# Scattering MoE results by node, keeping block marks, and adding index products on TensorE in a four-layer GNN with mixtures of experts

## The chip, the cores and the metric

The kernel runs on one core of a Trainium2 chip. The metric is device microseconds of one execution, the median of five runs. The engines are TensorE (PE, with its weight loads as PEld), VectorE (DVE), ScalarE (ACT), GpSimd (POOL) and SyncE (SP). DMAs are issued from SP's, ACT's and POOL's queues; a DMA whose rows go to or come from places given by a list of indices is an indirect DMA and is issued by POOL, 128 rows in each.

## The reference, cut to what matters

N = 3125 nodes hold rows of D = 256 floats. Eight layers follow one another, each added to the rows after a layer norm:

```python
x = x + L0_gnn(ln(x), edge_weight, src, dst)       # weighted sum over 50000 edges
x = x + L0_ffn(ln(x))      # 8 experts, top 2, hidden 512, relu
x = x + L1_gnn(ln(x))      # two graph attentions with 4 heads, W 256x256
x = x + L1_ffn(ln(x))      # tokens + 8 experts, top 2, hidden 256, gelu
x = x + L2_gnn(ln(x))      # normalised weighted sum, then a two-layer MLP
x = x + L2_ffn(ln(x))      # scores by a graph attention, 4 experts, top 2
x = x + L3_gnn(ln(x))      # two mean aggregations
x = x + L3_ffn(ln(x))      # 8 experts, top 2, hidden 1024, gelu
```

A mixture of experts (MoE) picks for each node the two experts e with the largest gate values and forms

```python
out[node] = w0 * (act(x[node] @ W1[e0] + b1[e0]) @ W2[e0] + b2[e0]) \
          + w1 * (act(x[node] @ W1[e1] + b1[e1]) @ W2[e1] + b2[e1])
```

The edges come sorted by dst. One layer of the kernel needs them in the other order too, by the block of 128 nodes to which src belongs.

## The kernel before, in words

The nodes lie in T = 25 tiles of P = 128; `X` in on-chip memory holds all of them. The stages run in the order of the layers; look preparation of edge lists comes first. The tile framework puts the instructions of each engine into an order when the program is built, and each engine then runs its own list in that order, with semaphores between them.

**The other graph's places (`own_places`, L1795 to L1820).** For 128 x 512 edge slots the kernel computes the slot in a table sorted by block. For each block b of 25 a mark (`op_B`: is the edge in block b, L1803) is scanned to a running count (`op_S`, L1804); the mark is used once and its buffer given back. In a second loop the mark is made again (L1816), multiplied with the count and the block's offset (`op_q`, L1817), and added to a sum `op_f` (L1819). All this is DVE's. `os_at` (L1820) is the result as integers.

**Sending the edge records (`own_send`, L1826).** 512 indirect DMAs on POOL write 128 edge records each to their places in the table `os_table`. They are handed out in small numbers among other stages' work: 21 in look, 5 x 8 while the first buckets are filled, two after each of 100 source steps of r0_gnn and 12 in its last 25 steps, three a chunk in r0_ffn (84), nine in each of four attention tails, three or four a chunk in r1_ffn (98), and 21 behind r1_ffn. `os_mark` (L1838, in `settle`) is a read of the table ahead of a branch. `own_load` reads the table back as `fa_rec`.

**r0_gnn.** The 25 destination tiles are taken in five groups of five. For each group 25 source steps follow: `r_hs` and `r_hd` (L1549) on DVE, products `r_pw` (L1553) on PE, the copy `r_wt` (L1557) on ACT, the sums `r_pa` (L1521) on PE, and an addition to X (L1522). The dense blocks `r_wt` also go to `mats` in DRAM. Beside the first four groups the fields of the next group's buckets are filled, one bucket in five steps (`bf_rh`, L1473). In the fifth group the steps of the following MoE's gate are mixed in.

**The gate (`mix_group`, `mix_send`).** Token tiles are taken in six groups (5, 5, 5, 5, 4, 1): a layer norm into `gh_xn` (two buffers; L191, L206 on ACT for r0_ffn), gate values, the top two experts with weights `gd_w`, and places `gd_at`. For each expert there is a region of rows in the DRAM tensor `regions`; each tile's rows are sent there by two indirect DMAs on POOL (L869, 50 in each MoE). `clear` (L100) zeros `regions` at the beginning by 26 DMAs of 1 MB on SP.

**The experts (`gated`).** Three MoEs (r0_ffn, r1_ffn, r3_ffn) use it. Chunks of 256 rows of a region are taken: rows `gx_xs` (L987) and weights `gx_w` arrive by SP; PE turns the rows over (`gx_pt`, L997), DVE copies them (`gx_xt`, L999); PE and ACT compute `gx_h` (L1004, L1005); and one chunk later `second` computes `gx_po` (L974) and, on DVE, `gx_ys` (L976). A DMA on ACT's queue (L977) puts the 256 result rows at place k x 256 of `ff_results`, in the order of chunks. 28 chunks run always; four more stand in a branch that this input does not take. For the places, 25 x 8 small arrays (`gd_adj`, `gd_q`, `gd_qs`) turn `gd_pos` into rows of `ff_results`, and three DMAs of 1 MB write zeros to the four chunks in the branch.

**Bringing the results back (`mix_result`, L1035).** For each tile and each of the two experts an indirect DMA (L360, `gb_y`) on POOL collects 128 rows of `ff_results`, and DVE adds `w * y` to X:

```python
y = pool.tile([P, D], F32, name="gb_y")
self.gather(y, m.results, m.at[i][:, t:t + 1])
nc.vector.scalar_tensor_tensor(self.X[:, t, :], y, m.w[i][:, t:t + 1], self.X[:, t, :], op0=OP.mult, op1=OP.add)
```

In r0_ffn and r1_ffn this is done in the next stage (r1_gnn, r2_gnn) group by group, followed by the norm and the first product (`hd_hx` there, `r_xw` here) of the group. In r3_ffn it is the end of the program, with the output DMAs.

In r1_gnn the two attentions collect rows by 832 indirect DMAs on POOL (L360, `ad_rows` from `r_rows`).

## Time and profile before

| what | value |
|---|---|
| median of five runs | 4864.8 us (4862.15 to 4866.09) |
| the profiled execution | 4864.93 us, of it the traced span 4863.1 us |
| PE busy | 3445.5 us (71%), 20909 instructions |
| DVE busy | 2862.3 us (59%), 9396 instructions |
| ACT busy | 2152.2 us (44%) |
| POOL busy | 2103.1 us (43%), 2107 instructions |
| os_table, L1826 POOL | 512 sends, 551.2 us, mean 1077 ns |
| regions rows, L869 POOL | 150 sends, 150.3 us, mean 1002 ns |
| gb_y, L360 POOL | 150 gathers, 154.8 us, mean 1032 ns |
| ad_rows from r_rows, L360 POOL | 832 gathers, 820.1 us, mean 986 ns |
| mean granted TensorE clock | 0.845 |

Busy times are shares of one span that has many stages with different limits; a stage has to be read by its own stretch. In the lines of the profile, `L360 POOL DMA_INDIRECT gb_y<-ff_results,gd_at x150` is a line of the kernel, an engine, an operation, what it writes and reads, and how many there are; `<-` behind a time names what ended the wait. Stretches are named by their bounds in us from the start of the span, as in 84:124. A row of the table by stage has the length, the busy time of each engine with its number of instructions, the granted PE clock, the share of the DMA engines' time and the GB/s that they moved.

### The profile page before, as it was taken

The page shows a single profiled execution, that of the slowest core. Times are in us where ns is not written, and L with a number is a line of the kernel's source. Part 1 is how long each engine was busy: PE and PEld are TensorE (multiplying, and loading weights), DVE is VectorE, ACT ScalarE, POOL GpSimd, SP SyncE. Part 2 cuts the span into 40 slices and gives each one's busy share as a digit, 9 for nine tenths or more (in the row PEclk, how much of TensorE's full clock was granted, in tenths as well). Part 3 has the DMA queues.
Part 4 walks back from the last instruction along what each step waited for, and adds up shares of the span by engine and source line. Part 5 has one row for each costly group of instructions (what it writes and reads, how often), then busy time and mean ns, then how long its engine had stood idle before and what let it go on. Part 6 is the DMA issues. An engine that isn't in the chain of part 4 may idle for free. (4 is left out here: it accounts for less than half of the span.)

```text
span 4863.1 us, 66173 instructions
## 1 busy us (share of the span) xinstructions
PE 3445.5 (71%) x20909; PEld 2770.8 (57%) x20909; DVE 2862.3 (59%) x9396; ACT 2152.2 (44%) x5957; POOL 2103.1 (43%) x2107
## 2 busy tenths in 40 slices
PE   1299988934666445545637877677877999979993
PEld 1189976823444334434525766444545888868883
DVE  7988863255666457766337876567778785231112
ACT  3366552225766456666114987333334332112220
POOL 0586533357777577775573000277770000120003
PEclk9699988966777667776878988788988999989996
DMA  1552226634545244443642222211110112325554
GB/s 58 167 167 96 96 106 196 219 109 135 145 140 145 66 134 136 131 129 89 190 132 94 109 82 82 54 36 32 36 30 6 67 62 81 104 95 199 187 193 132
DMA packets 329438, 543.00 MB, mean 112 GB/s; under 512 B 69070, under 2 KB 242002, under 8 KB 325872
## 3 DMA queue, kind: packets, MB, share of 16 engines
q1 hardware_dynamic: 213430, 354.48, 21.6%
q0 software_dynamic: 84032, 154.27, 12.1%
q10 hardware_dynamic: 31610, 29.84, 1.8%
q8 instruction: 173, 2.83, 0.2%
q14 instruction: 193, 1.58, 0.1%
HBM read 393.49 MB, written 145.37 MB: 111 GB/s over the span
## 5 line engine op out<-in xcount | busy, mean ns | idle before, releaser
L360 POOL DMA_INDIRECT ad_rows<-r_rows,fa_gi x832 | 820.1, 986 | 277.5 <-issue 241.3
L1826 POOL DMA_INDIRECT os_table<-os_rec,os_at x512 | 551.2, 1077 | 548.1 <-ACT gx_h L1005 152.4
L360 POOL DMA_INDIRECT ad_rows<-q_rows,own_gi x416 | 401.7, 966 | 633.5 <-DVE ad_hb L2104 510.4
L2213 ACT ACTIVATE ad_rows<-ad_rows 128x64 f32<-128x64 f32 x2544 | 617.0, 334 | 1.6
L2223 PE MATMUL ad_acc<-ad_rows,ad_hd 128*128 128x260 f32 x1664 | 519.7, 466 | 6.6 <-ACT ad_rows L2213 5.9
L869 POOL DMA_INDIRECT regions<-gh_xn,gd_at x150 | 150.3, 1002 | 738.8 <-PE r_pa L1654 544.9
L1654 PE MATMUL r_pa<-r_xs,r_cnt 128*128 128x257 bf16 (+1 forms) x3750 | 450.0, 273 | 0.9 <-ACT r_xs L1627 0.9
L1005 ACT ACTIVATE gx_h<-gx_pa,gx_bias 128x256 f32<-128x256 f32 x392 | 185.8, 474 | 571.3 <-PE gx_pa L1004 546.1
L2223 PEld LDWEIGHTS ad_acc<-ad_rows,ad_hd 128*128 128x128 f32 x1664 | 368.0, 233 | 73.6 <-ACT ad_rows L2213 11.2
L976 DVE TENSOR_TENSOR gx_ys<-gx_po,gx_b 128x256 f32<-128x256 f32 x168 | 70.6, 423 | 548.3 <-PE gx_po L974 528.6
L1654 PEld LDWEIGHTS <-r_cnt 128*128 128x128 bf16 x3750 | 362.2, 98 | 48.5 <-issue 0.2
L2126 PE MATMUL ad_pt<-ident,ad_e 128*4 128x128 f32 x75 | 26.2, 349 | 498.7 <-DVE ad_e L2123 407.5
L1004 PE MATMUL gx_pa<-gx_xt,gx_w 128*128 128x256 f32 x1568 | 364.7, 387 | 3.5 <-DMA gx_w<-in_L_ffn_W 2.3
L974 PE MATMUL gx_po<-gx_w,gx_h 128*128 128x256 f32 x1568 | 365.8, 379 | 0.0
L360 POOL DMA_INDIRECT gb_y<-ff_results,gd_at x150 | 154.8, 1032 | 482.8 <-SPq L126 438.9
L1004 PEld LDWEIGHTS gx_pa<-gx_xt,gx_w 128*128 128x128 f32 x1568 | 293.9, 192 | 68.0 <-DVE gx_xt L999 18.9
L974 PEld LDWEIGHTS gx_po<-gx_w,gx_h 128*128 128x128 f32 x1568 | 290.1, 190 | 38.1 <-ACT gx_h L1005 2.2
L1521 PE MATMUL r_pa<-r_xn,r_wt 128*128 128x257 f32 x1250 | 301.0, 386 | 14.3 <-ACT r_wt L1557 13.0
L2126 PEld LDWEIGHTS ad_pt<-ident,ad_e 128*4 128x4 f32 x75 | 6.1, 82 | 531.1 <-issue 497.7
L2600 PE MATMUL ss_sum<-r_xw,ss_wt 128*128 128x256 f32 x1250 | 290.0, 394 | 6.2 <-DMA ss_wt<-mats 6.2
L2600 PEld LDWEIGHTS ss_sum<-r_xw,ss_wt 128*128 128x128 f32 x1250 | 245.6, 198 | 41.7 <-issue 6.6
L2112 ACT CAST ad_hd<-ad_hb 128x2176 f32<-128x2176 bf16 (+1 forms) x50 | 98.4, 1968 | 355.0 <-PE ad_acc L2223 265.4
(573 smaller groups left out, 7133.9 us busy)
## 6 DMA issues: line engine op xcount, KB each, us to landing
gx_w<-in_L_ffn_W SPq DMA_DIRECT2D x56, 1024.0 KB
mats<-r_wt SPq DMA_DIRECT2D x25, 1600.0 KB
ss_wt<-mats SPq DMA_DIRECT2D x25, 1600.0 KB
gx_w<-in_L_ffn_W SPq DMA_DIRECT2D x56, 512.0 KB
regions<-zero SPq DMA_DIRECT2D x26, 1024.0 KB
ad_rb<-fa_relT SPq DMA_DIRECT2D x48, 544.0 KB
gx_xs<-regions SPq DMA_DIRECT2D x84, 256.0 KB
ff_results<-gx_ys ACTq DMA_DIRECT2D x84, 256.0 KB
```

The lines of the kernel that those rows point to most:

```text
L360: return self.nc.gpsimd.indirect_dma_start(out=out, out_offset=None, in_=table[:, :], in_offset=bass.IndirectOffsetOnAxis(ap=idx, axis=0))
L869: ins = nc.gpsimd.indirect_dma_start(out=self.regions[:, :], out_offset=bass.IndirectOffsetOnAxis(ap=m.at[i][:, t:t + 1], axis=0), in_=x, ...
L974: nc.tensor.matmul(po, h[:, f, j * P:(j + 1) * P], w2s[:, f, :], start=f == 0, stop=f == FC - 1)
L1004: nc.tensor.matmul(ps, w1s[:, c, f * P:(f + 1) * P], xt[:, c, :], start=c == 0, stop=c == DC - 1)
L1005: done = nc.scalar.activation(h[:, f, :], ps, act, bias=bias1[:, f, k:k + 1])
L1521: nc.tensor.matmul(pa, wt[:, i, :], xn[:, g * G + i, :], start=i == 0, stop=i == G - 1)
L1654: nc.tensor.matmul(pa[:, 0:n], c[:, u, :], xs[i][:, u, j, 0:n], start=u == 0 and j == 0, stop=u == T - 1 and j == 2)
L1826: i = nc.gpsimd.indirect_dma_start(out=s.table[:, :], out_offset=bass.IndirectOffsetOnAxis(ap=s.at[:, c:c + 1], axis=0), in_=s.rec[:, c, : ...
L2112: nc.scalar.copy(x.hd[:, :x.kb, :], x.hb[:, :x.kb, :])
L2213: i = nc.scalar.activation(v, v, AF.Copy, scale=x.rt[:, k, W4 + h:W4 + h + 1])
L2223: nc.tensor.matmul(x.acc, lhs[:, k, :], rhs[:, k, :], start=i == 0, stop=i == x.kb - 1)
L2600: nc.tensor.matmul(sums[t], wt[:, d, :], xw[:, d, :], start=d == 0, stop=d == T - 1)
```

## The change

1. Rows that go to `regions` get a 257th column, a number that holds the MoE, the node and the second of its two experts. It is made by three small DVE operations for each group in `mix_group`. `clear` and the loads of `gx_xs` have 257 columns too.
2. In `gated`, a new function `places` computes from that column, by seven small DVE operations for each chunk, at which row of a DRAM tensor of 8192 rows (4096 for each of the two experts of a node, in the order of nodes) each result belongs. `second` sends `gx_ys` there by two indirect DMAs for each chunk on POOL. The ACT DMA, the small arrays for the places and the zeros of the branch's chunks are gone; two small DMAs zero the 75 rows behind the last node.
3. `settle` also reads one element of the results, before the branch and after it.
4. `mix_results` brings the results back by plain DMAs on SP, two for each group of tiles and up to three groups ahead, in place of 50 indirect DMAs on POOL. The DVE additions are as before.
5. The numbers of `own_send` change: three instead of two after each of r0_gnn's first 100 steps, seven instead of nine in the attention tails, one a chunk instead of three or four in r1_ffn. With these all 512 are sent by the 27th chunk of r1_ffn, and the reads of `own_load` come ahead of r1_ffn's branch on SP.
6. `own_places` keeps its 25 marks, and the 25 products are added up by TensorE: a matmul with the identity for each, into one PSUM tile. `op_q` has two buffers.

```diff
-        self.regions = self.dram.tile([8 * RC, D], F32, name="regions")
+        self.regions = self.dram.tile([8 * RC, D + 1], F32, name="regions")
...
+            self.nc.sync.dma_start(self.landed, self.landing[0:1, 0:1])
...
+        e1 = hp.tile([P, TG, E], F32, name="gh_e1")[:, :G, :]
+        nc.vector.tensor_tensor(e1, s1, m.far[:, None, :].to_broadcast(all_), OP.mult)
+        nc.vector.tensor_reduce(rows[:, :, D], e1, AX.X, OP.add)
+        nc.vector.tensor_add(rows[:, :, D], rows[:, :, D], m.tag[:, gs])
...
-                    nc.scalar.dma_start(results[k * CH:(k + 1) * CH, :].rearrange("(j p) d -> p j d", p=P), y)
+                        i = nc.gpsimd.indirect_dma_start(
+                            out=results[:, :], out_offset=bass.IndirectOffsetOnAxis(ap=to[:, j:j + 1], axis=0),
+                            in_=y[:, j, :], in_offset=None, bounds_check=2 * HALF - 1, oob_is_err=False)
...
+                def places(k, xs):
+                    code = xs[:, :, D]
+                    ci_ = yp.tile([P, CJ], I32, name="gx_ci")
+                    nc.vector.tensor_scalar(ci_, code, float(-TAG * m.n), None, op0=OP.add)
...
+                    to = yp.tile([P, CJ], I32, name="gx_to")
+                    nc.vector.tensor_tensor(to, half, ci_, OP.add)
+                    return to
...
                         nc.vector.tensor_copy(xt, pt)
+                        to = places(k, xs)
...
-                        if k == 3:
-                            nc.scalar.dma_start(results[KA * CH:K * CH, :].rearrange("(q p) d -> p q d", p=P),
-                                                self.zero[:, None, 0:D].to_broadcast([P, (K - KA) * CJ, D]))
...
+    def mix_results(self, m, pool):
+        nc, ys = self.nc, []
+        groups = list(GROUPS)
+        def fetch():
+            g, n = groups.pop(0)
+            y = pool.tile([P, 2, TG, D], F32, name="gb_y")
+            for i in range(2):
+                nc.sync.dma_start(y[:, i, 0:n, :], m.results[i * HALF + g * P:i * HALF + (g + n) * P, :].rearrange("(t p) d -> p t d", p=P))
+            ys.append(y)
+        for g, n in GROUPS:
+            while groups and len(ys) < 3:
+                fetch()
+            y = ys.pop(0)
+            for t in range(n):
+                for i in range(2):
+                    nc.vector.scalar_tensor_tensor(self.X[:, g + t, :], y[:, i, t, :], m.w[i][:, g + t:g + t + 1],
+                                                   self.X[:, g + t, :], op0=OP.mult, op1=OP.add)
+            yield g, n
...
-                    self.own_send(2 if g < T // G - 1 else src % 2, done)
+                    self.own_send(3 if g < T // G - 1 else src % 2, done)
...
+            B = pool.tile([P, T, C], BF16, name="op_B")
+            for b in range(T):
+                nc.vector.tensor_scalar(B[:, b, :], blk, float(b), None, op0=OP.is_equal)
...
-                B = p2.tile([P, C], BF16, name="op_B")
-                nc.vector.tensor_scalar(B, blk, float(b), None, op0=OP.is_equal)
-                nc.vector.scalar_tensor_tensor(q, S[:, b, :], off[:, b:b + 1], B, op0=OP.add, op1=OP.mult)
-                if b:
-                    nc.vector.tensor_add(f, f, q)
-            nc.vector.tensor_scalar_add(s.at, f, NOWHERE)
+                q = p2.tile([P, C], F32, name="op_q")
+                nc.vector.scalar_tensor_tensor(q, S[:, b, :], off[:, b:b + 1], B[:, b, :], op0=OP.add, op1=OP.mult)
+                nc.tensor.matmul(acc, self.ident, q, start=b == 0, stop=b == T - 1)
+            nc.vector.scalar_tensor_tensor(s.at, drop, NOWHERE / 64.0, acc, op0=OP.mult, op1=OP.add)
...
-                self.own_send(9, i)
+                self.own_send(7, i)
...
-        self.gated(self.mix, "L1_ffn_w1", "L1_ffn_b1", "L1_ffn_w2", "L1_ffn_b2", AF.Gelu, send=3, more=2, tail=False)
+        self.gated(self.mix, "L1_ffn_w1", "L1_ffn_b1", "L1_ffn_w2", "L1_ffn_b2", AF.Gelu, send=1, tail=False)
```

## Prediction

> **What bounds it now.** The profiled execution took 4864.9 us (span 4863.1, the rest lies around it); the median of the runs is 4864.8, so the sum below is made against 4864.9. No engine bounds the whole span, so I read the table by stage first: the stretches that the change touches.
>
> ```profile
> core 0: us, PE busy (x) PEld busy (x) DVE busy (x) ACT busy (x) POOL busy (x), PEclk, DMA share, GB/s
> 84.00:124.00 40.00, 1.43 (x14) 1.06 (x14) 39.91 (x80) 1.61 (x3) 0.00 (x0) 1.00 0.31 92
> 200.00:280.00 80.00, 46.90 (x323) 42.56 (x323) 77.86 (x165) 60.25 (x166) 65.68 (x48) 0.75 1.00 318
> 240.00:640.00 400.00, 392.88 (x2594) 358.78 (x2593) 342.68 (x903) 238.84 (x668) 246.71 (x223) 0.99 0.35 120
> 760.00:980.00 220.00, 213.90 (x1019) 179.59 (x1017) 49.27 (x109) 55.14 (x113) 81.61 (x84) 0.99 0.70 221
> 980.00:1080.00 100.00, 39.45 (x152) 28.57 (x152) 65.66 (x200) 25.86 (x63) 54.82 (x52) 0.69 0.42 117
> 2340.00:2480.00 140.00, 121.09 (x560) 92.48 (x560) 40.91 (x84) 27.75 (x57) 93.65 (x97) 0.98 0.77 234
> 2480.00:2620.00 140.00, 45.11 (x150) 32.11 (x150) 84.05 (x178) 31.38 (x75) 95.57 (x98) 0.63 0.23 60
> 4786.00:4863.00 77.00, 0.00 (x0) 0.00 (x0) 24.36 (x51) 0.00 (x0) 47.32 (x50) 0.53 0.43 132
> ```
>
> Look preparation (84:124) is DVE alone; r0_gnn (240:640) and the MoE chunks (760:980, 2340:2480) are PE; the three stretches behind the chunk loops are nobody's: POOL is busy for about two thirds at most and DVE waits. Next, what ends the wait there (groups by tile, the end of the program; then the waits of 2480:2620):
>
> ```profile
> L360 POOL DMA_INDIRECT gb_y<-ff_results,gd_at x50: 942/946/982, 4792.6 to 4853.9; - x50
> L1035 DVE SCALAR_TENSOR_TENSOR X<-gb_y,gd_w,X x50: 483/485/486, 4795.5 to 4857.3; 128x256 f32<-128x256 f32 x50
> ```
> ```profile
> DVE X L1035 <- DMA gb_y<-ff_results,gd_at: 42.2, 16, 25.1
> ```
>
> 50 gathers take 61.3 us from first to last, 1.25 each (0.95 busy, 0.30 issue), and DVE is done 3.4 us after the last. The 25.1 is one stop: after four gathers POOL sends 21 edge rows (2490.7 to 2517.3) and the other 46 gathers queue behind.
>
> Last, POOL in r0_gnn (groups of two stretches; two rows of the timeline):
>
> ```profile
> L1826 POOL DMA_INDIRECT os_table<-os_rec,os_at x80 | 95.3, 1191 | 25.6 <-issue 20.1 <-ACT r_wt L1557 2.4 <-ACT bf_hr L1465 1.5
> L1826 POOL DMA_INDIRECT os_table<-os_rec,os_at x113 | 114.0, 1009 | 83.4 <-ACT r_wt L1557 60.9 <-issue 22.2 <-ACT bf_hr L1465 0.3
> ```
> ```profile
> 347.86 2.38 DVE L1473 TENSOR_TENSOR bf_rh<-bf_h,bf_f 128x2125 bf16<-128x2125 bf16 x1 [0.55 <-PE bf_ps L1476]
> 348.02 3.06 POOL L1826 DMA_INDIRECT os_table<-os_rec,os_at  x1 [0.30 <-issue]
> ```
>
> In 280:400 sends run back to back; in 400:600 POOL waits 61 us for source steps, so two sends a step just fit. A lone send takes 0.97 + 0.30; the one that meets bf_rh takes 3.06. Five steps take 17.48 us (one bf_rh each, 365.33 after 347.86), and 12 sends fit: 1.457 each.
>
> **The change, part by part.**
>
> *Marks kept, products added by TensorE.* The second loop takes 39.8 us: 25 marks of 0.423, 25 products of 0.750 and 24 sums of 0.691 on DVE. Afterwards DVE has the products and one last operation (19.5 us) and waits for TensorE, since only two product tiles exist. A 128x512 f32 sum is two matmul records; the nearest shape, q_a L2728, has 384 records busy 190.5 us, 0.50 each, so 0.99 a product, 25 us. Result 39.8 - 25.8 = -14. Ends: DVE-bound -20; at q_a's slowest record (1.222, two of them, 2.44 a product, 61 us) +21. I take -14, as the clock row of this very stretch is 1.00 with PE nearly idle. The Trainium skill (TensorE: Matmul & The Clock Gate, part 1) speaks against that: after an idle window of about 3.4 us the array runs at half speed until as long a busy one. By it PE would start this loop at half speed, and the term would be about -12 or worse; the row 84:124 does not show it, 160:180 (clock 0.50) does.
>
> *The zeros.* clear() writes 26 MB in 200:280 at 318 GB/s with the DMA full. 3.1 MB of result zeros ahead of it go (-10 us), and rows become 1028 bytes. Nearest row: attention gathers of 1040-byte rows, 141 GB/s at share 0.49 = 288, against 132 at 0.43 = 307: 7% of 82 us, +6. Since r0_gnn's end turns out to be POOL's (below), I count 0. The Trainium skill (DMA: Bandwidth & Descriptors, How a descriptor splits into AXI transactions) says that a descriptor off a 256-byte boundary fetches from the boundary below. An estimate from it: 37 beats for 32, +13 us here.
>
> *r0_gnn, three sends a step instead of two.* 100 more sends come ahead of the first row send on POOL (before: 647.0). 340 sends are due by the end of the fourth group (597), first at 198. By 280 49 are out (the row of 200:280 has 48). From 280 to 597, 317/1.457 = 218. Left 73, and 8 of the last twelve: 81 x 1.275 = 103, until about 700: the row sends start 54 us late. What waits: ACT's gh_xn L191 of the third token group (662.8; already 4.9 us behind the first group's row sends, as gh_xn has two buffers), and behind it on ACT every r_wt copy, so PE too. One of those waits of 4.9 is absorbed: +49. The lower end, every send at 1.275 from 280 on: 299 x 1.275, 661, 14 late, +9. I keep the nearest row, 1.457, as bf_rh stays.
>
> *Chunk loop.* Per chunk: no ACT result DMA, but seven tiny DVE operations (about 1 us; DVE idles 70% there) and two scatters on POOL (2.55 us). gx_to has two buffers: writing it in chunk k+1 waits until the scatters of k-1 landed, and ys of k queues behind it on DVE. The loop: one scatter 1.25, landing 2.8 (gather rows of the chain), gx_to 0.2, two ys 0.84: 5.1 us. r1_ffn's period is 5.03: about +2, with jitter +4 over 28 chunks. Ends: ACT stops waiting for the result DMA (25.1 us, 6 times), down to -20; one edge send ahead and a late landing, 6.4 us, +38. r0_ffn's period is 7.9 and POOL needs 5 x 1.275 = 6.4: +3 (0 to +10). r3_ffn's 14.5 hides it: 0. The tag costs three small DVE operations a group, of which the last group's are exposed, 1 us for each of three MoEs: +3.
>
> *Results fetched in node order.* At the end: last ys at 4785.8, scatter and landing 4790, branch 3.3 (as 977.69 to 980.98) and two reads on SP, first fetch 4794 to 4796. 6.55 MB of results and 3.2 MB of output at 307 GB/s take 32 us, DVE 50 x 0.40 = 20 in that shadow; with 5.8 from the last X to the end, 4828 to 4832: -33 (-22 if SP starts late, -38). Ahead of r1_gnn DVE becomes the bound: first data about 992, 53 us of DVE work until the last X at 1057.4 before: 1045, less 3 for hand-overs: -9 (-16 to +2).
>
> *r2.* No send is left there (the last 27 go one a chunk in r1_ffn, where 98 went before), and fa_rec's reads move on SP ahead of r1_ffn's branch. First fetch about 2486, data 2491, then 80 of DVE's 84 us: last r_xw about 2577, before 2614: -37 (-25 to -42).
>
> *Attention tails, 9 to 7 sends.* The second attention's rows are ready at 1669 (last r_rows 1667.1), POOL sends until 1688.4: 8 x 1.275 = -10 (0 to -10).
>
> Sum without r0_gnn: -14 + 3 + 3 - 9 - 10 + 4 - 37 - 33 = -93. With it, -93 + 49 = -44: 4821 us.
>
> **Rivals.**
> - *The backlog drains at the free rate*, because sends only stretch in the full DMA of 200:280: +9 instead of +49, 4781 us. For it: a lone send is 0.97. Against: the 3.06 beside bf_rh.
> - *The scatter loop bounds the chunks*: period 6.0 in r1_ffn, 28 x 0.97 = +27 for +4, and +10 for +3 in r0_ffn: 4851 us. For it: PE of r1_ffn is busy only 121 of 140 already. Against: 5.1 against 5.03.
> - *TensorE stays slow in the sums*: +21 for -14, 4856 us. Against: clock 1.00.
> - *Slower: POOL's queue in r0_gnn takes all back.* The gains of 93 are gone when the row sends start 98 us late, at 745: a mean of (745 - 198)/348 = 1.572 us a send. If the backlog keeps the 82/49 = 1.67 of the stretch 198 to 280: 779, +127, 4899 us. For it: ACT in its order holds PE, so nothing hides the lag. Against: 1.50 at most in 280:400, where the DMA share is 0.3.
>
> **How the numbers follow.** Forecast 0.40, free rate 0.20, scatter loop 0.14, slow TensorE 0.07, POOL queue 0.14, something unseen 0.05. About 0.2% (10 us) can be told from no change. Faster: 0.40 + 0.20 + 0.14, half of the slow-TensorE case (it lies on the edge) and half of the unseen: 0.80; slower the POOL queue's 0.14 and 0.01 of the unseen: 0.15; same the rest, 0.05. The range runs from 4775, below the free rate's 4781, to 4862, over the scatter loop and slow TensorE; left out are the POOL queue and tails.
>
> **What would show it.** Right: POOL busy without a wait for r_wt until about 690, the first regions row there, a wait of some 50 us of ACT gh_xn L191 on its DMA; the stretch after r1_ffn without os_table and DVE full; 30 us between the last ys and the end's X instead of 71; op_acc matmuls near 0.5 us a record. Wrong: row sends before 665 (then 4781); ys waiting for gx_to with a period over 5.5 in r1_ffn; a first gb_y fetch later than 12 us after the last ys; PE clock 0.5 in the sums. The prediction fails upward if r0_ffn starts later than 90 us after its old time less the 14 of the look.

## The result, and the profile after

The changed kernel takes 4867.7 us (median of 25 runs, 4859.6 to 4876.2), the kernel before 4865.6 beside it: ratio 1.0006 [1.0000, 1.0011], no change that could be told. A later comparison (e17 below) gave 4870.5 against 4864.9, 1.0012 [1.0002, 1.0021]. The prediction was 4821 with a range of 4775 to 4862: wrong, on the slow side, 5.7 us over the end of its range.

The profiled execution of after took 4876.2 us (span 4874.4), the longest of its runs, so its ledger ends 11.3 us late. The table follows landmarks of the program in both traces. "Own" is what the section between two landmarks adds; the column sums to 11.3.

| landmark | before | after | late by | own | predicted |
|---|---|---|---|---|---|
| first source step of r0_gnn (`r_hs`) | 236.2 | 226.7 | -9.5 | -9.5 | -14 (look) |
| first row to `regions` | 647.0 | 713.3 | +66.3 | +75.8 | +54 (backlog), zeros 0 |
| first `gx_xs` of r0_ffn | 756.7 | 822.1 | +65.4 | -0.9 | -5 (a wait absorbed) |
| last `gx_ys` of r0_ffn | 976.7 | 1067.6 | +90.9 | +25.5 | +3 |
| first attention gather | 1082.5 | 1160.4 | +77.9 | -13.0 | -9 |
| last attention gather | 2259.8 | 2333.7 | +73.9 | -4.0 | -10 |
| first `gx_xs` of r1_ffn | 2337.4 | 2411.5 | +74.1 | +0.2 | 0 |
| last `gx_ys` of r1_ffn | 2478.1 | 2575.8 | +97.7 | +23.6 | +4 |
| last `r_xw` of r2_gnn | 2617.5 | 2666.5 | +49.0 | -48.7 | -37 |
| first `gx_xs` of r3_ffn | 4372.7 | 4420.2 | +47.5 | -1.5 | 0 |
| last `gx_ys` of r3_ffn | 4785.8 | 4833.8 | +48.0 | +0.5 | 0 |
| end of the span | 4863.1 | 4874.4 | +11.3 | -36.7 | -33 |

Three rows are far off: the way to the row sends, and two chunk loops. The table by stage of the profile after shows the same places (length, then busy us and instructions of PE, PEld, DVE, ACT, POOL; granted PE clock, DMA share, GB/s):

```profile
core 0: us, PE busy (x) PEld busy (x) DVE busy (x) ACT busy (x) POOL busy (x), PEclk, DMA share, GB/s
84.00:132.00 48.00, 30.26 (x78) 10.88 (x79) 41.45 (x65) 2.06 (x3) 0.00 (x0) 0.87 0.26 77
173.00:300.00 127.00, 49.98 (x344) 45.55 (x344) 96.91 (x188) 69.43 (x188) 90.77 (x69) 0.65 1.11 212
822.00:1068.00 246.00, 223.74 (x1015) 184.14 (x1013) 67.34 (x304) 55.03 (x113) 133.96 (x138) 0.96 0.63 195
2411.00:2576.00 165.00, 128.66 (x560) 98.12 (x560) 62.43 (x280) 28.36 (x58) 78.73 (x81) 0.93 0.65 196
2576.00:2670.00 94.00, 42.91 (x150) 31.10 (x150) 75.94 (x179) 30.93 (x75) 21.99 (x27) 0.73 0.30 93
4834.00:4874.00 40.00, 0.00 (x0) 0.00 (x0) 20.31 (x51) 0.00 (x0) 0.97 (x1) 0.54 0.75 247
```

The last two rows are the gains: behind r1_ffn DVE is busy for 76 of 94 us where it was for 84 of 140, and the end takes 40 us where it took 77, with POOL out of it. The second row is a surprise: the DMA engines are as full as before (a share of 1.11 for 1.00) and move 212 GB/s where they moved 318. In the two chunk loops (third and fourth row) PE, which was busy 214 of 220 and 121 of 140, now has holes.

What fills the holes (waits of three stretches of after: the clearing 130:330, the last row sends 640:822, then r0_ffn 822:1068 and r1_ffn 2411:2576; in all, times, longest, us):

```profile
ACT r_wt L1603 <- DMA mats<-r_wt: 45.3, 1, 45.3
ACT gh_xn L199 <- DMA regions<-gh_xn,gd_at: 51.1, 3, 40.4
DVE gx_to L1010 <- DMA ff_results<-gx_ys,gx_to: 149.0, 26, 7.7
DVE gx_to L1010 <- DMA ff_results<-gx_ys,gx_to: 80.1, 26, 5.9
```

The first is new and nowhere in the prediction: the first dense blocks cannot be written to `mats` while `regions` are being cleared, ACT stands for 45 us, and PE with it. It follows from the clearing itself (groups by tile, SP's 26 DMAs, before and then after; name, count, shortest/median/longest of an issue in ns, first and last):

```profile
L100 SPq DMA_DIRECT2D regions<-zero x26: 587/3205/6337, 186.2 to 265.1; - x26
L104 SPq DMA_DIRECT2D regions<-zero x26: 534/4895/6953, 173.1 to 287.6; - x26
```

From the first issue to the last it is 114.5 us for 78.9, with 0.4% more bytes.

The second wait is the predicted one of about 50 us: POOL's backlog. The first row send stands straight behind the last edge send of r0_gnn (POOL's timeline; start, length, what, idle before it):

```profile
712.05 0.97 POOL L1871 DMA_INDIRECT os_table<-os_rec,os_at  x1 [0.30 <-issue]
713.32 0.97 POOL L888 DMA_INDIRECT regions<-gh_xn,gd_at  x1 [0.30 <-issue]
```

The third and the fourth are the scatter loop. Two rows of DVE's timeline in r1_ffn show how it bites:

```profile
2482.57 0.16 DVE L1010 TENSOR_TENSOR gx_to<-gx_half,gx_ci 128x2 int32<-128x2 f32 x1 [4.80 <-DMA ff_results<-gx_ys,gx_to]
2482.65 0.42 DVE L989 TENSOR_TENSOR gx_ys<-gx_po,gx_b 128x256 f32<-128x256 f32 x1
```

A 0.16 us operation that nobody needs for several microseconds stands for 4.80 until an older scatter is through with its buffer, and `gx_ys`, whose scatters are the next in the chain, stands behind it in DVE's order. The period is 8.8 us a chunk in r0_ffn (before 7.9) and 5.9 in r1_ffn (before 5.0).

At the end of the program, the groups by tile answer to the two lines shown of before:

```profile
L1070 SPq DMA_DIRECT2D gb_y<-ff_results x12: 391/1485/2065, 4841.7 to 4857.2; - x12
L1079 DVE SCALAR_TENSOR_TENSOR X<-gb_y,gd_w,X x50: 480/480/486, 4846.7 to 4866.3; 128x256 f32<-128x256 f32 x50
```

Twelve plain reads are issued in 15.5 us where 50 gathers took 61.3, and DVE's fifty additions take 20 us.

### The profile page after: what moved, and what is told of

Same layout as the page of the kernel before. It is cut to its first block, busy times and chain, and to the rows that moved or that the text cites. A ratio compares the mean times of both kernels' runs of the same rounds, so it can differ in the third digit from the quotient of the medians.

```text
span 4874.4 us, 66796 instructions
## 1 busy us (share of the span) xinstructions
PE 3486.2 (72%) x20959; PEld 2791.6 (57%) x20959; DVE 2894.9 (59%) x9958; ACT 2150.0 (44%) x5957; POOL 2135.2 (44%) x2131
## 5 line engine op out<-in xcount | busy, mean ns | idle before, releaser
L1871 POOL DMA_INDIRECT os_table<-os_rec,os_at x512 | 574.6, 1122 | 462.9 <-ACT gx_h L1040 150.9
L1700 PEld LDWEIGHTS <-r_cnt 128*128 128x128 bf16 x3750 | 362.0, 98 | 48.7 <-issue 0.2
L990 POOL DMA_INDIRECT ff_results<-gx_ys,gx_to x168 | 163.5, 973 | 410.7 <-DVE gx_ys L989 376.5
L1567 PEld LDWEIGHTS r_pa<-r_xn,r_wt 128*128 128x128 f32 x1250 | 229.7, 193 | 113.2 <-ACT r_wt L1603 85.5
```

The source lines that it names most:

```text
L990: i = nc.gpsimd.indirect_dma_start(out=results[:, :], out_offset=bass.IndirectOffsetOnAxis(ap=to[:, j:j + 1], axis=0), in_=y[:, j, :], in_ ...
L1567: nc.tensor.matmul(pa, wt[:, i, :], xn[:, g * G + i, :], start=i == 0, stop=i == G - 1)
L1700: nc.tensor.matmul(pa[:, 0:n], c[:, u, :], xs[i][:, u, j, 0:n], start=u == 0 and j == 0, stop=u == T - 1 and j == 2)
L1871: i = nc.gpsimd.indirect_dma_start(out=s.table[:, :], out_offset=bass.IndirectOffsetOnAxis(ap=s.at[:, c:c + 1], axis=0), in_=s.rec[:, c, : ...
```

## The experiments

My theory after this: the gains came as predicted, and three costs ate them, (a) the rows of 1028 bytes in the clearing, (b) the backlog of edge sends in r0_gnn, (c) DVE's order in the chunk loops. The main rivals: that the sends or POOL's own load, not the order, cost the time in (c), and that a cost taken away in one place comes back in another.

The chips of e1 to e13, e18 and e19 take 5640 to 5700 us for the kernel before too. DVE, ACT and POOL are busy as long there, to about 1%; PE is busy some 5% longer (3630 us in the part of e5 that is the kernel before, for 3446), the mean granted clock is 0.79 to 0.80 for 0.845, and the rest is idle time. e14 to e17 ran on a chip like the first (4865). So ratios are against the kernel before on the same chip, and times of stages are best compared within a chip: e1, e2, e3 and e5 share one, e6 to e9 another, e10 to e13 a third, e18 and e19 a fourth.

One thing about the slower chips bears on all that follows. The kernel before takes 220.2 us (e5) and 220.7 (e13) in r0_ffn there, as on the first chip, but 176.4 and 178.3 in r1_ffn, where the first chip takes 140.7; and its first row send is at 668.3 (e5). So the changed kernel's r1_ffn (160.1 in e6) is shorter than before's on such a chip, the times of r1_ffn that the expectations name were taken from the first chip, and what the change loses there is lost at the row sends (784.4 in e6) and in r0_ffn (245.2).

### One cost at a time: e1, e2, e3, e6, e7, e8

**e1_old_sends** puts back the old numbers of edge sends:

```diff
-                    self.own_send(3 if g < T // G - 1 else src % 2, done)
+                    self.own_send(2 if g < T // G - 1 else src % 2, done)
-                self.own_send(7, i)
+                self.own_send(9, i)
-        self.gated(..., AF.Gelu, send=1, tail=False)
+        self.gated(..., AF.Gelu, send=3, more=2, tail=False)
```

> The changed kernel with the numbers of own_send of before (two a step in r0_gnn, nine in the attention tails, three or four a chunk in r1_ffn, the rest behind it). Theory (POOL's backlog in r0_gnn holds ACT for 40 us): that wait of ACT gh_xn on its DMA falls below 6 us, the first row send comes at 675 to 685 instead of 713 (it stays behind the 637 that look's gain would allow, because the clearing of regions still stalls PE), and r0_ffn's first chunk loads 30 to 36 us earlier. Given back later: in r1_ffn POOL has 5.5 operations a chunk, 7.0 us against a period of 5.9, +30, and the attention tail +6. Total near the changed kernel, 4862 to 4875. Rival (the clearing alone makes r0_gnn late, POOL only follows): first row send stays at 705 to 715, total 4885 to 4905.

Measured: 5718.0 us, ratio 1.0061 [1.0042, 1.0080]. The first row send is at 690.8, where e2 and e3 on the same chip have 778.8 and 805.4: the sends set the time of the row sends, which is cost (b). The `gh_xn` wait on its DMA, by which the backlog showed on the first chip, cannot be used here: it is 3.9 us in e1, and with three sends a step it is just as short on these chips (3.9 in e6, 8.6 in e3). And r1_ffn takes 235.0 us, against 166.4 in e2: three or four edge sends a chunk and two scatters are five or six POOL operations of 1.27 us, some 7 us of a chunk that now takes 8.4. The time came back there.

**e2_flat_clear** writes the same zeros from a tile that holds 8 x 257 of them in each partition, so that a descriptor writes 8224 bytes in a row:

```diff
-            self.nc.sync.dma_start(v[q], self.zero[:, None, 0:D + 1].to_broadcast([P, 8, D + 1]))
+            wide = pool.tile([P, 8 * (D + 1)], F32, name="wide")
+            nc.gpsimd.memset(wide, 0.0)
+            v = self.regions.rearrange("(q p r) d -> q p (r d)", p=P, r=8)
+            for q in range(v.shape[0]):
+                nc.sync.dma_start(v[q], wide)
```

> The changed kernel, but regions are cleared from a tile of 2056 zeros a partition, so that each partition's 8 rows are one run of 8224 bytes; nothing else differs. Theory (rows of 1028 bytes slow the DMA engines: 211 GB/s against 318 for 1024): the clearing takes 80 to 88 us instead of 114, PE's stall of 45 us on the mats DMA falls to 7 to 10. But POOL's backlog sets the end of r0_gnn anyway, so the row sends start at 695 to 705 instead of 713 and the total falls by only 8 to 18 us, 4850 to 4860. Rival 1 (the stall is what counts): total falls by 35 to 40, 4828 to 4833. Rival 2 (another traffic in that stretch, not the row length, makes the rate 211): no change in the clearing's 114 us, total 4865 to 4870.

Measured: 5717.4, ratio 1.0057 [1.0033, 1.0081]. The clearing (groups by tile of e2) takes 51 us, less than half of after's and less than before's 79:

```profile
L1551 SPq DMA_DIRECT2D regions<-wide x26: 332/340/1885, 175.2 to 226.0; - x26
```

**e3_deep** gives the small tiles and the results of a chunk four buffers:

```diff
-                    tc.tile_pool(name="gx_h", bufs=2) as hp, tc.tile_pool(name="gx_y", bufs=2) as yp, \
+                    tc.tile_pool(name="gx_h", bufs=2) as hp, tc.tile_pool(name="gx_y", bufs=4) as yp, \
```

> The changed kernel with four buffers instead of two for gx_ys and the seven little tiles of places. Theory (the wait of gx_to and gx_ys for the landing of the scatters of two chunks ago bounds the chunks): the waits of gx_to on its DMA (149 us in r0_ffn, 80 in r1_ffn) vanish, r0_ffn falls from 245 to 220 to 226 us, r1_ffn from 164 to 141 to 150; total 4820 to 4832. Rival (POOL's five operations a chunk or the loads of 1028-byte rows bound the chunks): the wait only changes its name, r0_ffn stays over 238 and r1_ffn over 158; total 4858 to 4868.

Measured: 5738.6, ratio 1.0095 [1.0066, 1.0123]; r0_ffn 258.2, r1_ffn 151.2. e2, whose chunk loops are those of the changed kernel, took 248.9 and 166.4 on this chip: with four buffers r1_ffn is 15 us shorter and r0_ffn is not shorter at all. There was no run of the changed kernel itself here, so the next three repeat it with the changed kernel beside them: **e6_after_again** is the changed kernel, **e7_deep_again** has e3's edit, **e8_flat_again** e2's.

> The changed kernel itself beside the kernel before, as the base for the others of this group. On a chip like that of the first measurement: 4865 to 4870 against 4865. On a chip like that of the first experiments (kernel before 5682, nearly the same busy times, but PE with gaps between its instructions): between 5715 and 5760.

> The changed kernel with four buffers instead of two for gx_ys and the little tiles of places, as before, to be compared with the changed kernel of this group. Theory (the scatter loop bounds the chunks): 35 to 47 us below the changed kernel where PE runs without gaps, r0_ffn 220 to 226 us and r1_ffn 141 to 150; less where PE itself is slow. Rival (POOL's five operations or the loads bound the chunks): 0 to 10 below.

> The changed kernel with regions cleared in runs of 8224 bytes, to be compared with the changed kernel of this group. The clearing takes 51 us as in the first group (it was 114 in the changed kernel). Theory (POOL's backlog sets the end of r0_gnn): the PE stall goes, but the first row send comes only 8 to 18 us earlier, total 8 to 18 below the changed kernel. Rival (the stall is what counts): 35 to 45 below.

| | us | ratio | first row send | r0_ffn | r1_ffn |
|---|---|---|---|---|---|
| e6, as after | 5688.5 | 1.0089 [1.0072, 1.0106] | 784.4 | 245.2 | 160.1 |
| e7, four buffers | 5670.5 | 1.0059 [1.0038, 1.0080] | 784.7 | 240.8 | 149.8 |
| e8, flat zeros | 5664.3 | 1.0043 [1.0026, 1.0059] | 764.3 | 246.6 | 163.9 |

The flat zeros bring the row sends 20 us and the program 24 us ahead. The expectation's theory had 8 to 18 and its rival 35 to 45; it lies between. It is the size of what the ledger of after leaves over at the row sends (75.8 - 54 = 22): cost (a) is shown. Four buffers bring 18 us, between theory and rival too, of which the loops are 15; but in r0_ffn the wait only changed its name (waits of e7):

```profile
DVE gx_ci L1000 <- DMA gx_xs<-regions: 100.6, 23, 5.9
```

`places` now stands ahead of `gx_ys` for the next chunk's rows, not for the old scatters. If this holds the loop, more buffers cannot mend it: work that needs the next chunk is issued ahead of work that ends this one. e10 tests that.

### What a row of 1028 bytes costs: e5

**e5_row_sizes** is the kernel before with eight more writes of 8.4 to 10.5 MB behind the output, by rows of 256, 257, 260, 272, 320 floats, then the flat form, then 512 and 514:

```diff
+        for k, w in enumerate((256, 257, 260, 272, 320, 0, 512, 514)):
...
+                    nc.sync.dma_start(v[q], flat[:, None, 0:w].to_broadcast([P, r, w]))
```

> The kernel before, and behind its output further writes to unused DRAM from one tile, 4 to 9 MB each, one after the other: rows of 1024, 1028, 1040, 1088 and 1280 bytes, then one run of 8224 bytes a partition, then rows of 2048 and 2056 bytes; they add about 130 us behind the end of the work. Theory (a row that isn't a multiple of some larger unit costs extra): 1024 about 318 GB/s, 1028 about 210, 1040 between 210 and 290, 1088 and 1280 near 300, 8224 over 300, 2048 about 320, 2056 about 250. Rival (the slow clearing came from other traffic): 1028 within 5% of 1024.

The DMA view of 5670:5770 and 5770:5884, GB/s in 40 slices each:

```profile
GB/s 138 108 308 178 343 340 305 190 178 213 194 201 197 190 190 214 200 179 192 211 205 202 200 215 256 247 213 300 300 293 290 285 286 284 281 332 349 352 352 353
```
```profile
GB/s 351 352 352 352 358 388 395 395 393 392 391 382 385 384 424 427 421 413 416 421 416 381 380 379 384 382 379 382 380 379 286 286 281 290 311 279 312 294 239 38
```

In the order of the writes: the end of the 1024-byte rows at about 340, then 1028 bytes about 200 (17 slices), 1040 about 290, 1088 352, 1280 about 392, 8224 bytes in a row about 418, 2048 381, and 2056 about 290. One float more than 1024 bytes costs 40% of the rate and two more than 2048 a quarter; 1088 and 1280 bytes, longer still, cost nothing. So it is not the number of bytes. Which lengths are slow beyond those written here, and whether the length of a row or the place at which it starts decides, these writes do not tell apart. Before's clearing had the first rate (318 with other traffic beside it), after's the second (212).

### Putting the savings together: e9, e10, e11, e12, e18, e19

**e12_spread_only** is the changed kernel with other numbers of sends: 11 in five source steps of r0_gnn, 12 at each group of r1_gnn's beginning, one or two a chunk in r1_ffn.

```diff
-                    self.own_send(3 if g < T // G - 1 else src % 2, done)
+                    self.own_send((3 if src % 5 == 0 else 2) if g < T // G - 1 else src % 2, done)
                 for g, n in self.mix_results(self.mix, bp):
+                    self.own_send(12)
-        self.gated(..., AF.Gelu, send=1, tail=False)
+        self.gated(..., AF.Gelu, send=1, more=2, tail=False)
```

> The changed kernel with only the numbers of own_send altered: 11 for five steps in r0_gnn, 12 for each group of tiles at the start of r1_gnn, one and two a chunk in r1_ffn; the clearing and the chunks stay. Theory (clearing and POOL's backlog hide each other in r0_gnn, so that each mended alone brings less than both): the wait of ACT gh_xn falls under 6 us; the row sends come 45 to 75 us earlier than in the changed kernel, against 20 with the flat clearing alone and 117 with both. Rival (backlog alone): 95 to 117 earlier. Given back in r1_ffn 5 to 15.

Measured: 5692.2, ratio 0.9986 [0.9974, 0.9998]; first row send 694.9; r0_ffn 248.0, r1_ffn 170.0. e10 below, on the same chip and with the sends of the changed kernel, has its first row send at 787.8: the sends alone bring it 93 us ahead, beyond the 45 to 75 of the theory and close to the rival's 95 to 117. The wait of `gh_xn` (waits of e12, 600:830) is small, but it is 8.5 us in e10, so it is not what got shorter here:

```profile
ACT gh_xn L199 <- DMA regions<-gh_xn,gd_at: 5.1, 1, 5.1
```

**e9_all** has e2's and e3's edits and e12's sends (10 in place of 12, and up to three a chunk in r1_ffn).

```diff
+                nc.sync.dma_start(v[q], wide)
+                    tc.tile_pool(name="gx_h", bufs=2) as hp, tc.tile_pool(name="gx_y", bufs=4) as yp, \
+                    self.own_send((3 if src % 5 == 0 else 2) if g < T // G - 1 else src % 2, done)
+                    self.own_send(10)
+        self.gated(..., AF.Gelu, send=1, more=3, tail=False)
```

> The changed kernel with all three mended: regions cleared in runs of 8224 bytes, four buffers for gx_ys and places, and own_send at 11 for five steps in r0_gnn (two, and one more at each fifth step), 10 for each group of tiles at the start of r1_gnn, where POOL is now idle, and one to three a chunk in r1_ffn. Theory (three separate costs took the gains): row sends back at 635 to 645 (-70), r0_ffn -22, r1_ffn -15 to -22: 4755 to 4785 where PE runs without gaps. Rival (the costs hide each other, or the gains behind the chunks never came): 4820 to 4860.

Measured: 5620.4, ratio 0.9954 [0.9938, 0.9969]; first row send 667.1; r0_ffn 257.3, r1_ffn 185.2. Against e6's ratio this is -1.35%; the three edits alone gave -1.03 (e12, on another chip), -0.46 (e8) and -0.30 (e7), 1.79 together. At the row sends they add (117 us, for 93 and 20), and do not hide each other, as the theory of e12 had it. But neither chunk loop came down by the 15 to 22 us expected: r0_ffn is 12 us longer than e6's, and r1_ffn, with up to two more sends a chunk, 25.

**e10_late_places** issues the seven operations of `places` after both `gx_ys` of the chunk before, with four buffers for the results and three for the rows; **e18_late_again** repeats it on another chip.

```diff
-                        to = places(k, xs)
...
-                        if last:
-                            second(*last)
+                        ys = second(*last) if last else None
+                        with tc.issue_after(ys.ins) if ys else nullcontext():
+                            to = places(k, xs)
```

> The changed kernel with four buffers for gx_ys and the little tiles of places, three for gx_xs, and the seven operations of places put behind the two gx_ys additions of the chunk before in DVE's order. Theory (what bounds the chunks is the order on DVE: first gx_to waited for scatters ahead of gx_ys, with deeper buffers gx_ci waits there for the load of the next chunk, whose SP queue waits for gx_po and gx_ys): with gx_ys ahead of gx_ci, r0_ffn takes 220 to 226 us (245 in the changed kernel, 241 with deep buffers alone), r1_ffn 141 to 147 (160 to 164; 150). Rival (POOL or the loads of 1028-byte rows): r0_ffn over 236, r1_ffn over 148.

Measured: 5722.4, ratio 1.0042 [1.0022, 1.0062]; r0_ffn 260.1, r1_ffn 153.8. DVE no longer waits for scatters or rows in r0_ffn, and r0_ffn is no shorter (table by stage of e10, then its longest wait of DVE there):

```profile
916.00:1177.00 261.00, 226.03 (x1017) 189.93 (x1014) 71.08 (x304) 53.33 (x113) 134.56 (x139) 0.93 0.59 184
```
```profile
DVE gx_ys L989 <- PE gx_po L987: 122.1, 37, 6.5
```

DVE waits for PE now. e12 took 248.0 in r0_ffn on the same chip with the early order, and the kernel before takes 220: in r0_ffn the order on DVE was not what cost the time, a point for the rival. r1_ffn's 153.8 lies in the rival's range too, and four buffers with the early order took 151.2 (e3) and 149.8 (e7) on other chips: no run there shows a gain from the order beside that from the buffers.

> The run with late places once more, to be read on a chip like that of the hybrid run. Theory (the order on DVE bounds the chunks; POOL has room): r0_ffn 217 to 224 us, r1_ffn 131 to 140, total 4805 to 4825. Rival (scatters behind three sends a chunk hold r0_ffn even so): r0_ffn 235 to 260, r1_ffn 131 to 140, total 4830 to 4850. On a chip as in the second to fourth group the rival's 260 comes again and tells nothing new.

Measured: 5739.0, ratio 1.0086 [1.0062, 1.0110]; r0_ffn 265.5, r1_ffn 155.0. It fell on a chip that is slow like e10's, so it adds nothing but a second value.

**e11_best** is e10 with e2's zeros and e12's sends; **e19_all_late** is the same again.

```diff
+                nc.sync.dma_start(v[q], wide)
+                        with tc.issue_after(ys.ins) if ys else nullcontext():
+                            to = places(k, xs)
+                    self.own_send((3 if src % 5 == 0 else 2) if g < T // G - 1 else src % 2, done)
+                    self.own_send(12)
+        self.gated(..., AF.Gelu, send=1, more=2, tail=False)
```

> The run before with, too, regions cleared in runs of 8224 bytes and own_send at 11 for five steps in r0_gnn, 12 for each group of tiles at the start of r1_gnn, one and two a chunk by turns in r1_ffn. Theory (the three costs are all that stood against the gains): row sends 110 to 120 us ahead of the changed kernel's on a chip as in the second group, chunk loops 220 to 226 and 145 to 155; 1.0% to 2.0% below the kernel before. Rival (r1_ffn's sends and scatters fill POOL and hold the chunks): r1_ffn over 165 as in the run with all three mended (185), 0.3 to 0.6% below the kernel before.

> The changed kernel with all three costs mended (flat clearing, late places with deeper buffers, sends at 11 for five steps in r0_gnn and 12 for each group of tiles at the start of r1_gnn, one and two a chunk in r1_ffn), scatters in all three MoEs. Theory: look and clearing -30, r0_ffn within 5 of before, start of r1_gnn -13, r1_ffn -9, then -54 and -39: 4720 to 4760. Rival (r0_ffn held by scatters behind sends, and r1_gnn's first gathers behind 72 sends): 4765 to 4800.

Measured: 5679.1, ratio 0.9957 [0.9941, 0.9974], and 5667.3, ratio 0.9965 [0.9950, 0.9980]; r0_ffn 262.6 and 255.2, r1_ffn 178.0 and 177.7. No better than e9, and within the 0.3 to 0.6% of the rival of e11; r1_ffn is over 165 as that rival had it, with the added sends there.

### The sums alone: e13

**e13_sums_only** is the kernel before with only the sixth part of the change.

```diff
+            B = pool.tile([P, T, C], BF16, name="op_B")
...
-                nc.vector.scalar_tensor_tensor(q, S[:, b, :], off[:, b:b + 1], B, op0=OP.add, op1=OP.mult)
-                if b:
-                    nc.vector.tensor_add(f, f, q)
+                nc.vector.scalar_tensor_tensor(q, S[:, b, :], off[:, b:b + 1], B[:, b, :], op0=OP.add, op1=OP.mult)
+                nc.tensor.matmul(acc, self.ident, q, start=b == 0, stop=b == T - 1)
```

> The kernel before with the new own_places alone (marks kept, products added by TensorE); nothing else differs. Theory (DVE's look is shorter by the marks and sums, less the wait for PE): the clearing starts 8 to 12 us earlier, and as POOL's sends and PE both follow it, the total falls by 6 to 12 us (0.1 to 0.2%). Rival (the gain is hidden by the clearing's DMAs, which run on to the same end): 0 to 3 us.

Measured: 5678.0, ratio 0.9956 [0.9939, 0.9972], 25 us (give or take 9) below the kernel before. The clearing starts at 176.3, where it starts at 185.4 in e5, which shares that part with before: 9 us are seen at the place of the change, as expected. Where the rest of the 25 comes from stays open.

### Scatters and sends apart, on a chip like the first: e14, e15, e17

**e14_no_scatter** keeps the late places and the edge sends, and writes the results by a DMA on ACT's queue in the order of chunks; the scatters are left out, so results do not reach their nodes.

```diff
-                        i = nc.gpsimd.indirect_dma_start(
-                            out=results[:, :], out_offset=bass.IndirectOffsetOnAxis(ap=to[:, j:j + 1], axis=0),
...
+                    nc.scalar.dma_start(results[k * CH:(k + 1) * CH, :].rearrange("(j p) d -> p j d", p=P), y)
```

> The run with late places (four buffers, places behind gx_ys), but each chunk's 256 result rows go by one DMA on ACT's queue to the place of the chunk, as before; the two scatters are left out, so that results do not reach their nodes; loads of 1028-byte rows and the operations of places stay. Theory now (the scatters themselves hold the loop, by what they do to the other queues): r0_ffn 220 to 226, r1_ffn 141 to 150. Rival (loads of 1028-byte rows and the small operations): r0_ffn 238 to 262.

**e15_no_sends** keeps the late places and the scatters, and sends no edges in the chunks of r0_ffn and r1_ffn but 19 at each group of r1_gnn's beginning.

```diff
                 for g, n in self.mix_results(self.mix, bp):
+                    self.own_send(19)
...
-        self.gated(..., AF.Relu, beside=self.fill_edges, send=3, tail=False)
+        self.gated(..., AF.Relu, beside=self.fill_edges, tail=False)
-        self.gated(..., AF.Gelu, send=1, tail=False)
+        self.gated(..., AF.Gelu, tail=False)
```

> The run with late places, without edge sends in the chunks of r0_ffn and r1_ffn (19 for each group of tiles at the start of r1_gnn instead, so that r1_gnn starts later); scatters stay. Theory (scatters themselves): r0_ffn stays 238 to 262. Rival (five POOL operations a chunk, the scatters standing behind the sends): r0_ffn 220 to 228, r1_ffn 141 to 146.

**e17_after_third** is the changed kernel on the same chip.

> The changed kernel as the base of this group. On a chip as in the last groups 0.3 to 0.9% above the kernel before, r0_ffn 245 to 250 us, r1_ffn 160 to 170; on one like the first, equal to the kernel before within 0.2%.

| | us | ratio | r0_ffn | r1_ffn |
|---|---|---|---|---|
| before (first profile) | 4864.9 | | 220.0 | 140.7 |
| e17, as after | 4870.5 | 1.0012 [1.0002, 1.0021] | 242.3 | 164.9 |
| e14, no scatters | 4855.2 | 0.9978 [0.9966, 0.9989] | 217.0 | 149.9 |
| e15, no sends | 4899.0 | 1.0070 [1.0052, 1.0089] | 217.0 | 132.9 |

r0_ffn by stage, of e14 and of e15:

```profile
821.00:1039.00 218.00, 212.91 (x1017) 183.74 (x1014) 71.67 (x304) 55.05 (x113) 81.59 (x84) 0.97 0.73 225
```
```profile
820.00:1038.00 218.00, 212.69 (x1017) 184.03 (x1015) 72.21 (x304) 55.04 (x113) 53.46 (x55) 0.97 0.69 220
```

With late places, either one alone costs r0_ffn nothing: PE is busy 213 of 218 us. So the theory of e15, that scatters alone hold the loop, fell, and so did e14's rival, the loads of 1028-byte rows and the small operations. In the changed kernel POOL has both (134 us busy with 138 operations, in 246), and `places` comes early: that run differs from e14 and e15 in two things. Late places with both were run only on the slower chips, where they did not help (e10, 260.1). r1_ffn is another case: with late places and scatters, and no sends, it takes 132.9 us, 8 less than before. Of e14 only r0_ffn can be read: as its results do not reach their nodes, r2_gnn fetches them before r1_ffn is over, and r3_ffn goes through 32 chunks, not 28, so that its time in r1_ffn and its total stand beside no other run's. As a whole e15 is slower because the sends it moved stand ahead of the first attention's gathers (the first at about 1222, after's at 1160).

### A version that keeps the gains: e16

**e16_hybrid** leaves r0_ffn as it was before (results in the order of chunks, fetched by 50 gathers), where the chunks have three edge sends and the fetch in node order had gained 13 us for 25 lost in the loop. r1_ffn and r3_ffn scatter, with late places and the plain fetch. The zeros are flat, and the sends are spread: 11 in five steps of r0_gnn, 4 a chunk in r0_ffn, 9 in the tails, one or two a chunk in r1_ffn, the rest behind it.

```diff
+            direct = m.n == 1
...
+                        if direct:
+                            continue
...
+                        ys = second(*last) if last else None
+                        with tc.issue_after(ys.ins) if ys else nullcontext():
+                            to = None if direct else places(k, xs)
...
+                nc.sync.dma_start(v[q], wide)
...
+                    self.own_send((3 if src % 5 == 0 else 2) if g < T // G - 1 else src % 2, done)
```

> A version from what the runs showed: the changed kernel with flat clearing; r0_ffn as in the kernel before (results in chunk order by ACT's queue, gathers at the start of r1_gnn); r1_ffn and r3_ffn with scatters, late places and plain loads of the results; sends at 11 for five steps in r0_gnn, four a chunk in r0_ffn, nine in the attention tails, one and two a chunk in r1_ffn, the rest behind it. Theory: look -10, clearing -20, r0_ffn 220, r1_ffn within 10 of before, then -50 behind r1_ffn and -39 at the end: 90 to 120 us below the kernel before (1.6 to 2.2% on a chip as in the last groups). Rival (the gains behind r1_ffn are given back in the attention that follows): under 1%.

Measured: 4760.6 us (4755.7 to 4765.9), ratio 0.9785 [0.9772, 0.9799]: faster than both, and as the theory had it. r0_ffn takes 220.8 us with its four sends a chunk. r1_ffn by stage of e16:

```profile
2320.00:2452.00 132.00, 120.14 (x560) 92.47 (x560) 64.55 (x280) 27.74 (x57) 89.69 (x93) 0.97 0.80 241
```

POOL carries 93 operations here and PE is still busy 120 of 132: with late places and deeper buffers, one or two sends a chunk fit beside the scatters. The 104.3 us (span 4758.8) by the landmarks: 18.4 at the first row send (628.6), which is 20.8 at the first attention gather and 14.9 at the last; 47 over r1_ffn and r2's beginning (r1_ffn 131.5 for 140.7), 5.5 until the last `gx_ys` of r3_ffn, 36.8 at the end.

## Why the prediction was wrong

**The zeros: 0. This step failed.** The row taken for 1028-byte rows was that of gathers of 1040 bytes, 7% slower; the write at 1028 bytes measured 212 against 318 GB/s in the traces, about 200 against 340 in e5. The clearing took 35.6 us longer. The estimate that was made from the Trainium skill (DMA: Bandwidth & Descriptors, How a descriptor splits into AXI transactions), +13 us, had the right sign and a third of the size. Its rule does not account for these writes: rows of 1088 bytes too start off a 256-byte boundary three times in four, and they were written at 352 GB/s, no slower than rows of 1024 (e5). And the cover named for it (r0_gnn's end is POOL's) was not there: the clearing holds `mats`, `mats` holds `r_wt` on ACT, and with `r_wt` come the `done` of the edge sends. POOL's sends waited 11.9 us of it for ACT (200:340 of after). About 22 us at the row sends; 20 there and 24 of the total by e8, on a slower chip.

**Chunk loops: +3 and +4. This step failed by size.** They measured +25.5 and +23.6. The mechanism was on the page, wait and waiting queue, and even as a rival (the scatter loop, at +10 and +27). In r1_ffn the rival's number was right; the mistake was to call 5.1 against 5.03 a cover, when a loop as long as the period takes every late landing as a loss: the period became 5.9. e15 and e16 show that it is what `places` waits for on DVE: with `places` late and its buffers deeper, r1_ffn takes 132.9 and 131.5 us on a chip like the first. How much is the order and how much the buffers is not shown there; on slower chips the buffers alone bring 10 and 15 us (e7 against e6, e3 against e2). Then the loop is about 8 us shorter than before: part of the far end that I had given it (ACT without its result DMA, down to -20), though no run shows that this is its cause. In r0_ffn the sum of POOL's load, 5 x 1.275 = 6.4 of 7.9 us, was called hidden, and it isn't: e14 and e15 show that, with late places, sends alone or scatters alone are hidden, and after shows, with early places, that both together are not. On the slower chips late places did not mend it (e10), which speaks for POOL's load; how a POOL that is busy for 54% holds the loop, and whether late places with sends would do on a chip like the first, stays open.

**r0_gnn's backlog: right.** Between 340 and 600 of after a send takes 1.50 us. 1.457 us a send gave a first row send at 700 and 54 us of lateness; it was 713.3, directly behind the last edge send, with the clearing's 22 in it. The longest wait was 40 us, about 50 were predicted. The free-rate rival (4781) fell. On the first chip e16, with fewer sends a step and flat zeros, has its first row send at 628.6 and takes the wait from 51.1 to 15.6 us (18.6 before); on slower chips fewer sends a step bring the row sends 115 (e3 to e1) and 93 us (e10 to e12) ahead. e1 shows why the sends cannot merely go back: with the early places r1_ffn has no room for them and for scatters (235.0 us).

**The sums on TensorE: right in kind.** -9.5 at the first source step for -14. PE's idle time ahead of them all ended with DVE (groups of 84:132 of after; busy, mean ns of one, idle before and what ended it):

```profile
L1864 PE MATMUL op_acc<-op_q,ident 128*128 128x512 f32 x50 | 29.4, 713 | 11.9 <-DVE op_q L1863 11.9
```

The 0.59 us of busy time a record is a mean of two speeds (PE's timeline of the same stretch):

```profile
86.83 2.08 PE L1864 MATMUL op_acc<-op_q,ident 128*128 128x512 f32 x2 [0.87 <-DVE op_q L1863]
94.85 14.13 PE L1864 MATMUL op_acc<-op_q,ident 128*128 128x512 f32 x28
123.96 3.37 PE L1864 MATMUL op_acc<-op_q,ident 128*128 128x512 f32 x4 [10.24 <-DVE op_q L1863]
```

From 94.85 on records come every 0.50 us, as predicted. The first six, up to 92.7, come about every 1.0; PE had stood for 9.85 us until 85.17, shortly before them. So do the first three of the last four, behind 10.24 us of waiting, where the granted clock is 0.50 (118:126). The rule of the Trainium skill that was weighed there (TensorE: Matmul & The Clock Gate, part 1), half speed behind an idle window, is thus seen in this loop, and the row 84:124 of before with its clock of 1.00 did not speak against it: the trace has no record of a granted clock ahead of 141.1 there (ahead of 92.7 in after), and the view counts time without a record as 1.00. It cost little, as DVE waited for PE 5.3 us in all; so the rival of the slow TensorE (+21), which needed every record slow, fell.

**Plain fetches and r2: right, somewhat better.** -13.0 for -9, -48.7 for -37, -36.7 for -33; the DVE-bound reading held (76 of 94 us behind r1_ffn). The tails gave -4 for -10; r3_ffn nothing, as predicted.

With the two failed steps at their predicted size, 22 + 22.5 + 19.6 us less, the profiled execution would have been 4812. The range left it out since the rivals were taken one at a time: the scatter loop (+30) and a slow clearing, priced at nothing, came together.

## What to carry to other kernels

A wait costs what stands behind it in its engine's order, so small address arithmetic that reuses a buffer, or needs the next tile, should have buffers enough and stand behind the eviction that the pipeline waits for (both together took r1_ffn from 164.9 to 131.5 us, e17 to e16, though e16 sends more there; they were not tried apart on that chip); when a loop's latency equals its period, count it as exposed. When a row gets a tag column, price the new length in every transfer that uses it: here the added four bytes cost 35.6 us of clearing and nothing that could be seen in the loads (e14, 217.0 us in r0_ffn), and a contiguous source of zeros made the clearing cheaper than it had been. Work taken off a queue in one stage and given to the same queue in another is only a gain where that stage's queue has room beside everything else that the change puts there.

## What the runs showed of the hardware that was not expected

- Writes of rows of 1028 bytes ran at about 200 GB/s, those of 1024 at about 340, of 1040 at 290, of 1280 at 392, and runs of 8224 bytes at 418 (e5).
- The same kernel takes 4865 us on some chips and 5640 to 5700 on others, with a mean granted clock of 0.845 and of 0.79 to 0.80. r0_ffn takes 220 us on both, r1_ffn 140.7 and 176.4 to 178.3. The effect of the change differs with it: 1.0006 and 1.0012 on the former, 1.0089 on the latter (e6).
- A loop with PE busy for 213 us took 218 with POOL busy for 82 us or for 53 (e14, e15), and 261 with POOL busy for 135 (e10, the same order on DVE, a slower chip on which the kernel before takes 220).
